# Layer 0's excess nodes: own rows by a product on TensorE in place of a gather from memory

## The chip, the core and the metric

The kernel runs on one core of one Trainium2 chip. The metric is the device time of one execution in microseconds (us). A core has engines that each work through a queue of their own, in order: PE (TensorE, matrix products), DVE (VectorE), ACT (ScalarE), POOL (GpSimd, which here mainly issues gathers) and SP (SyncE, which issues transfers). They wait for one another by semaphores. Matrix products land in PSUM[...]; everything else lies in SBUF, 128 partitions wide, or in device memory.

## The reference

Four graph-attention layers over the same graph of 3327 nodes with 256 features, each followed by a residual sum and a layer norm. A node has few neighbours (about 1% of the entries of the adjacency are set). Only layer 0 concerns the change:

```python
g_src = nodes @ W_src_w.T + W_src_b
g_tgt = nodes @ W_tgt_w.T + W_tgt_b
g = g_src[:, None, :] + g_tgt[None, :, :]
g = jax.nn.leaky_relu(g, NEG_SLOPE)
score = jnp.einsum('ijc,c->ij', g, a_w)
score = jnp.where(adj_mat != 0, score, -jnp.inf)
weights = jax.nn.softmax(score, axis=1)
return weights @ g_tgt
...
x = _layernorm(x + _L0_gnn_ref(x, adj, ...), axis=-1)
```

The leaky ReLU stands inside the sum over features, so a score needs all 256 features of both nodes. Layers 1 to 3 have scores that are sums of a term of each node, and are computed densely.

## The kernel before, in words

Layer 0 (`sparse0`) works on neighbour lists. The 26 tiles of 128 nodes are cut into four sets of 4, 7, 9 and 6 tiles (`SETS`). For each set, `neighbours(s)` reads the adjacency, encodes it by small products on PE into banks of the PSUM ring `v` (three banks, `fill`, L548), lets DVE pick the indices (`scan`, `sort`, L572 to L592), counts them and ranks the nodes of the set by degree (`ranks_i`, L682). Nodes are then taken in order of rank, so that tile 0 of a set has the nodes with most neighbours. For sets 1 to 3 the lists go to memory and back (`write_list` L731, `read_lists` L739, on POOL).

A node gets a number of seats, its tile's (`LEVELS`). Tile 0 would need 56 (`KMAX`), but has only 42 to 44 (`SEATS`); the neighbours over that are handled together, in one further part per set: the *excess*. Each of its 128 rows is a pair of a node and one of its neighbours over the seats. `excess(s)` (L760) gives every such pair a row, with comparisons on DVE (`seat`) and products on PE (L803) that carry along, for each row, the neighbour's index, the node's own index, its place in the tile and which of its seats it is. From these it makes `back` (row to node) and its transpose `forth` (node to row), both 128x128 matrices of zeros and ones.

The work is a list of parts: four seats of one tile make a part (`cuts_of`), tile after tile in the order 1, 0, 2, 3 and so on, with the excess part put in ahead of the last three parts of tile 0. There are 237 parts. One loop (L1282) goes over them. In step q it runs, in this order: some steps of the next set's `neighbours`; everything that `due` holds for q; the gathers of part q + 8 (`LEAD`); and the scores of part q. The order in which the loop calls is the order of each engine's queue (the manual schedule).

- `gather(q)` (L902): for every seat of the part, one indirect transfer on POOL fetches 128 table rows of 260 floats (`table_d`: projected target, with the score's linear part behind it) into a buffer `g`, one of a ring of 22. At a tile's beginning `gather_own` (L892) fetches the 128 nodes' own rows of 773 floats (minus the source projection at 0, the input at 257, the own target at 513) into `own`, of which there are four buffers. It is called 11 steps ahead of the tile's first part.
- `score(q)` (L942): DVE takes the larger of the gathered row and minus the source (L932), multiplies by the weight row `a_ps` and sums (L938).
- `weights` (L966): maximum on DVE, exponentials on ACT.
- `combine` (L1003), spread over the 8 steps after the tile's end: ACT scales each gathered row by its weight (L1012), PE adds the rows up by products with the identity (L1015). Then the `g` buffers are free.
- `add_input` (L1035), 10 steps after the tile's end: DVE divides and adds the input (L1041 to L1048), which is the last reading of the tile's `own`. `put_back` (L1054), 3 steps on: POOL writes the rows to memory in their old places.

For the excess, `gather_excess` (L828) issues two indirect transfers on POOL: own rows of 773 floats by the node's index, into one of the four `own` buffers, and table rows by the neighbour's index. `score_excess` (L841) takes the larger of the two on DVE (`y_over`, L845), weights and sums it. `send_scores` (L855), one step on, returns the scores to tile 0's seats by a product with `back`; later `send_weights` and `combine_excess` do the same for weights and rows.

In set 3's stretch no `neighbours` runs; there the ring `v` serves the first products of layer 1 for finished tiles (`early_bank`, `turn_next` L1139, `project_next` L1148). Layers 1 to 3 follow and overlap the end of layer 0 by a little.

Of the kernel before, what the change touches and what calls it, by code (L numbers as in the profile page):

```python
# [8 lines left out]
F32 = mybir.dt.float32  # L9
BF16 = mybir.dt.bfloat16  # L10
I32 = mybir.dt.int32
U32 = mybir.dt.uint32
U16 = mybir.dt.uint16
AF = mybir.ActivationFunctionType
ALU = mybir.AluOpType
# [4 lines left out]
P = 128  # L20
# [7 lines left out]
KMAX = 56  # L28
# [18 lines left out]
OWN = 773  # L47
# [3 lines left out]
def gat_stack(  # L51
# [29 lines left out]
    nc = tc.nc  # L81
    n, dim = x.shape
# [24 lines left out]
    table_d = dram.tile([n + 1, ROW], F32, name="table_d")  # L107
# [170 lines left out]
    def sparse0(lost):  # L278
        GROUP, TURNS, LEAD, SPREAD = 4, 22, 8, 8
        starts = [sum(SETS[:s]) for s in range(len(SETS))]  # L280
        with ExitStack() as s0:
            find = s0.enter_context(tc.tile_pool(name="s_find", bufs=2))
            const0 = s0.enter_context(tc.tile_pool(name="s_const", bufs=1))
            io0 = s0.enter_context(tc.tile_pool(name="s_io", bufs=2))
# [94 lines left out]
            upto = find.tile([P, P], F32, name="upto", bufs=1)  # L379
# [12 lines left out]
            minus_own = const0.tile([P, nt], F32, name="minus_own")  # L392
            nc.vector.tensor_scalar_mul(minus_own, own_i, -1.0)
            EXTRA = KMAX - min(SEATS.values())
            ramp = marks[:, 0, 0:1]
            before = find.tile([P, P], F32, name="before", bufs=1)
            given = find.tile([P, EXTRA, 4], F32, name="given", bufs=1)

            def excess_constants():
                nc.vector.tensor_scalar(before, upto, ramp, None, op0=ALU.is_gt)  # L400
                nc.vector.tensor_scalar(
                    given[:, :, 2], minus_own[:, 0:1].to_broadcast([P, EXTRA]), -1.0, 1.0,
                    op0=ALU.mult, op1=ALU.add,
                )
                nc.vector.tensor_scalar(given[:, :, 3], upto[:, :EXTRA], 1.0, None, op0=ALU.add)

            counts = const0.tile([P, nt, len(pieces) + 2], F32, name="counts")
            nc.vector.memset(counts, 0.0)
# [1 line left out]
            own_d = [  # L410
                dram.tile([size * P, OWN], F32, name=f"own{s}_d") for s, size in enumerate(SETS)
            ]
# [342 lines left out]
            held = {}  # L755
            between = []

            extras = {}

            def excess(s):  # L760

                lst, first = listed[s][:, 0, :], seats[s, 0]
                width = KMAX - first
                over = extras[s] = {}
                temp = a_ps[:, dim + 1 :]
                nc.vector.tensor_copy(given[:, :width, 0], lst[:, first:KMAX])
                nc.vector.tensor_copy(
                    given[:, :width, 1], lst[:, KMAX : KMAX + 1].to_broadcast([P, width])
                )
                there = io0.tile([P, EXTRA], F32, tag="there", name="there", bufs=1)  # L770
                count = io0.tile([P, 2], F32, tag="count", name="count", bufs=1)
                nc.vector.tensor_scalar(
                    there[:, :width], given[:, :width, 0], 0.0, 0.0, op0=ALU.is_gt, op1=ALU.add,
                    accum_out=count[:, 0:1],
                )
                absent = over["absent"] = io0.tile([P, EXTRA], F32, tag="absent", name="absent", bufs=1)
                nc.vector.tensor_scalar(
                    absent[:, :width], there[:, :width], -1.0, FAR, op0=ALU.add, op1=ALU.mult
                )
                yield  # L780
                nc.tensor.matmul(temp[:, 0:1], before, count[:, 0:1], start=True, stop=True)  # L781
                yield
                nc.vector.tensor_scalar(
                    count[:, 1:2], temp[:, 0:1], -float(BASE), None, op0=ALU.add
                )
                at = nt + starts[s]
                nc.vector.tensor_scalar(
                    lost[:, at : at + 1], count[:, 0:1], count[:, 1:2], float(P - BASE),
                    op0=ALU.add, op1=ALU.is_gt,
                )  # L790
                nc.vector.scalar_tensor_tensor(
                    there[:, :width], there[:, :width], float(BASE), upto[:, :width],
                    op0=ALU.mult, op1=ALU.add,
                )
                nc.vector.tensor_scalar(
                    there[:, :width], there[:, :width], count[:, 1:2], None, op0=ALU.add
                )
                for e in range(width):
                    seat = io0.tile([P, P], F32, tag="key_diag", name="seat")
                    nc.vector.tensor_scalar(  # L800
                        seat, upto, there[:, e : e + 1], None, op0=ALU.is_equal
                    )
                    nc.tensor.matmul(  # L803
                        temp[:, 8:12], seat, given[:, e, :], start=(e == 0), stop=(e == width - 1)
                    )
                    if e % 3 == 1:
                        yield
                yield
                taken = io0.tile([P, 4], F32, tag="taken", name="taken", bufs=1)
                nc.vector.tensor_copy(taken, temp[:, 8:12])  # L810
                rows = over["rows"] = io0.tile([P, 2], U32, tag="taken_i", name="taken_i", bufs=1)
                nc.vector.tensor_copy(rows, taken[:, :2])
                back = over["back"] = io0.tile([P, P], F32, tag="back", name="back", bufs=1)
                nc.vector.tensor_scalar(
                    back, upto, 1.0, taken[:, 2:3], op0=ALU.add, op1=ALU.is_equal
                )
                which = over["which"] = io0.tile([P, EXTRA], F32, tag="which", name="which", bufs=1)
                nc.vector.tensor_scalar(
                    which[:, :width], upto[:, :width], 1.0, taken[:, 3:4],
                    op0=ALU.add, op1=ALU.is_equal,  # L820
                )
                yield
                nc.tensor.transpose(temp[:, 96 : 96 + P], back, ident)
                yield
                there_too = over["forth"] = io0.tile([P, P], F32, tag="forth", name="forth", bufs=1)
                nc.scalar.copy(there_too, temp[:, 96 : 96 + P])

            def gather_excess(s, q):  # L828

                over = extras[s]  # L830
                own = over["own"] = io0.tile([P, OWN], F32, tag="own", name="own_of", bufs=4)
                g = over["g"] = gath.tile(
                    [P, GROUP, ROW], F32, tag=f"g{(q + SHIFT) % TURNS}", name="g"
                )
                for dst, src, x in ((own, own_d[s], 1), (g[:, 0, :], table_d, 0)):
                    nc.gpsimd.indirect_dma_start(
                        out=dst, out_offset=None, in_=src[:, :],
                        in_offset=bass.IndirectOffsetOnAxis(ap=over["rows"][:, x : x + 1], axis=0),
                    )

            def score_excess(s):  # L841

# [285 lines left out]
            def early_bank():  # L1128
                return ps0.tile([P, BANK], F32, tag="v", name="early", bufs=3)
# [50 lines left out]
            next(first)  # L1180
            score_columns()
            excess_constants()
            waiting, turns = None, 0
            for it in range(nt):
# [28 lines left out]
            def at_step(q, what, *args):  # L1213
                due.setdefault(q, []).append(lambda: what(*args))

            def once_placed(q, what, *args):
                due_gathers.setdefault(q, []).append(lambda: what(*args))

            due_gathers = {}
            for q, (key, k0, _) in enumerate(parts):  # L1220
                if k0 == KMAX:
                    at_step(q + 1, send_scores, key[0])
                    at_step(q + 2, take_scores, key[0])
                if k0 == 0:
                    if key[1] == orders[key[0]][0]:
                        at_step(q, judge, key[0])
                        at_step(q, lay_out, *key)
                    else:
                        once_placed(q - 3, gather_own, *key)
                        at_step(q - 2, lay_out, *key)  # L1230
# [15 lines left out]
            for s, q in begins.items():  # L1246
                work, at = excess(s), max(q - 2, 0)
                for y in range(12):
                    at_step(at + y, go_on, work)
# [48 lines left out]
            for q in sorted(due):  # L1298
# [7 lines left out]
                op0=ALU.mult, op1=ALU.add,  # L1306
# [777 lines left out]
    lost = nodes.tile([P, 2 * nt], F32, name="lost")  # L2084
    nc.vector.memset(lost, 0.0)
    rest = sparse0(lost)
    with ExitStack() as rs:
        layers(rs, EARLY, rest)
# [75 lines left out]
```

## Time and profile before

| | us |
|---|---|
| median of 3 timed runs (lowest to highest) | 3398.66 (3390.78 to 3407.27) |
| the profiled execution | 2952.55 |
| its span, first to last instruction | 2950.7 |

| engine | busy us | share of the span | instructions |
|---|---|---|---|
| PE (products) | 2317.0 | 79% | 15862 |
| DVE | 2134.7 | 72% | 5615 |
| POOL | 992.3 | 34% | 1061 |
| ACT | 852.4 | 29% | 2381 |

One execution was profiled, and all durations come from it. A share of the span is a mean over stages that differ, so it says little of any one of them. In the profile's rows `g<-table_d,lst` reads: an instruction that writes tile g from table_d and lst; x894 is how often; then come busy us, the mean ns of one, and the idle time of the engine before them with what ended it ("issue" is idle time in which nothing is waited for). L912 is line 912 of the program.

### The profile page before, as it was taken

To read this page: it belongs to the slowest core of one execution; us is meant where nothing else is said; L and a number is where in the kernel's file an instruction comes from. 1 tells how busy PE (TensorE), PEld (TensorE's weight loads), DVE (VectorE), ACT (ScalarE), POOL (GpSimd) and SP (SyncE) were. 2 spreads that over 40 slices of the span, in tenths; PEclk is the share of its full clock that TensorE was granted. 3 is DMA by queue.
4 is the path that set the end of the run, shared out by engine and by line. 5 is a ranking of instruction groups with operands and counts; after the bars stand their busy time and mean duration, and the time that the engine had idled before them with its cause. 6 is when DMAs were issued, how large, how long until landed. Compare 5 with 4: busy or idle time off the path is not lost.

```text
span 2950.7 us, 45073 instructions
## 1 busy us (share of the span) xinstructions
PE 2317.0 (79%) x15862; PEld 1359.2 (46%) x15862; DVE 2134.7 (72%) x5615; ACT 852.4 (29%) x2381; POOL 992.3 (34%) x1061
## 2 busy tenths in 40 slices
PE   7466667556545416657899999999999999999997
PEld 4222323222222103325688888763546567534332
DVE  6789789968776518755455521138999999999997
ACT  3244445434334304533344411110010110111211
POOL 2676767777777777772000000000000000000000
PEclk8576777777767757889999999999999999999998
DMA  7685655545644435545776733331222222212211
GB/s 234 194 263 147 187 166 171 141 130 158 166 112 114 112 107 124 171 120 165 227 208 195 201 82 107 110 98 45 73 61 84 75 80 63 73 43 62 59 47 48
DMA packets 183854, 370.50 MB, mean 126 GB/s; under 512 B 35772, under 2 KB 124707, under 8 KB 182596
## 3 DMA queue, kind: packets, MB, share of 16 engines
q1 hardware_dynamic: 103994, 178.49, 21.4%
q0 software_dynamic: 51008, 155.70, 19.1%
q10 hardware_dynamic: 28618, 33.33, 3.3%
q8 instruction: 128, 2.10, 0.3%
q14 instruction: 106, 0.87, 0.1%
HBM read 327.52 MB, written 46.23 MB: 127 GB/s over the span
## 4 chain that ended last, share of the span: by engine, by line
PE 46%; DVE 4%; DMA 2%; issue 0%; ACT 0%; SPq 0%; DVEq 0%; POOL 0%; POOLq 0%; ACTq 0%
PE acc L1773 18%; PE acc L1723 16%; PE acc L1781 9%; DVE e L1629 3%; PE misc L1557 3%; DMA at<-at_d 1%; PE misc L1666 0%; DMA at_d<-at 0%; DMA at_i<-in_adj_t_dram 0%; DVE stats L1952 0%; DVE h L1950 0%; DVE h L1745 0%; DVE both L1947 0%; PE misc L1822 0%; DMA dst<-in_l_att_dram 0%
## 5 line engine op out<-in xcount | busy, mean ns | idle before, releaser
L912 POOL DMA_INDIRECT g<-table_d,lst x894 | 851.6, 953 | 273.1 <-issue 245.6
L1629 DVE SCALAR_TENSOR_TENSOR e<-rate,feat,at 128x896 f32<-128x896 f32 (+4 forms) x832 | 843.6, 1080 | 59.2 <-PE acc L1781 47.7
L1015 PE MATMUL acc<-g,ident 128*128 128x512 f32 (+1 forms) x896 | 505.5, 708 | 262.3 <-ACT g L1012 246.1
L1773 PE MATMUL acc<-e,feat 128*32 128x384 f32 (+2 forms) x6656 | 692.7, 515 | 6.7 <-DVE h L1745 4.2
L1773 PEld LDWEIGHTS acc<-e,feat 128*32 128x32 f32 x6656 | 307.1, 110 | 300.2 <-issue 161.5
L1015 PEld LDWEIGHTS acc<-g,ident 128*128 128x128 f32 x896 | 195.1, 228 | 481.6 <-ACT g L1012 364.6
L1781 PE MATMUL acc<-e,feat 128*32 128x384 f32 (+3 forms) x3328 | 383.3, 512 | 0.0
L1012 ACT ACTIVATE g<-g,w 128x256 f32<-128x256 f32 x883 | 365.4, 495 | 0.4 <-ACT minus L489 0.4
L932 DVE TENSOR_TENSOR y<-g,minus_ps 128x1028 f32<-128x1028 f32 (+2 forms) x233 | 273.4, 1173 | 125.0 <-DMA g<-table_d,lst 115.9
L938 DVE SCALAR_TENSOR_TENSOR y<-y,a_ps 128x257 f32<-128x257 f32 x894 | 324.3, 418 | 24.8 <-PE a_ps L781 6.2
L1723 PE MATMUL acc<-feat,e 128*128 128x257 f32 (+2 forms) x1352 | 303.5, 382 | 9.1 <-DVE inv L1744 6.4
L1723 PEld LDWEIGHTS acc<-feat,e 128*128 128x128 f32 (+2 forms) x1352 | 254.9, 191 | 46.9 <-issue 9.3
L1723 PE MATMUL acc<-feat,at 128*128 128x257 bf16 (+2 forms) x2028 | 237.9, 274 | 4.2 <-DMA at<-at_d 4.0
L1781 PEld LDWEIGHTS acc<-e,feat 128*32 128x32 f32 (+1 forms) x3328 | 162.0, 110 | 130.8 <-issue 88.1
L1723 PEld LDWEIGHTS <-at 128*128 128x128 bf16 (+2 forms) x2028 | 198.8, 99 | 38.0 <-DMA at<-at_d 4.5
L553 PE MATMUL v<-code,leads 65*128 65x512 bf16 (+1 forms) x182 | 83.1, 458 | 156.9 <-DVE cand L579 111.0
L1629 DVE SCALAR_TENSOR_TENSOR e<-rate,feat,at_i 128x896 f32<-128x896 f32 (+2 forms) x104 | 112.3, 1081 | 92.1 <-DMA at_i<-in_adj_t_dram 44.6
L579 DVE MAX8 cand<-v 128x8 f32<-128x104 f32 (+2 forms) x858 | 158.9, 260 | 21.7 <-PE v L556 21.7
L1609 POOL DMA_DIRECT2D rate3b_d<-rate_rows x4 | 2.1, 520 | 449.8 <-ACT rate_rows L1608 449.8
L251 POOL TENSOR_TENSOR rstds<-rstds,minus_half 128x7 f32<-128x7 f32 (+1 forms) x8 | 12.0, 1506 | 385.0 <-DVE rstds L250 385.0
L1959 POOL TENSOR_TENSOR rstds<-rstds,minus_half 128x7 f32<-128x7 f32 (+1 forms) x4 | 7.6, 1912 | 384.5 <-DVE rstds L1958 384.5
L1656 ACT CAST at<-at_i 128x896 bf16<-128x896 int32 (+2 forms) x104 | 92.1, 885 | 111.9 <-DMA at_i<-in_adj_t_dram 75.5
(253 smaller groups left out, 1864.6 us busy)
## 6 DMA issues: line engine op xcount, KB each, us to landing
adj_i<-in_adj_dram SPq DMA_DIRECT2D x75, 512.0 KB
at<-at_d SPq DMA_DIRECT2D x150, 224.0 KB
at_i<-in_adj_t_dram SPq DMA_DIRECT2D x50, 448.0 KB
at<-at_d SPq DMA_DIRECT2D x75, 192.0 KB
at<-at_d SPq DMA_DIRECT2D x75, 191.8 KB
g<-table_d,lst POOLq DMA_INDIRECT x894, 2.8
at_d<-at ACTq DMA_DIRECT2D x50, 224.0 KB
at_i<-in_adj_t_dram SPq DMA_DIRECT2D x25, 384.0 KB
```

Of the source, the lines that this page charges most:

```text
L579: nc.vector.max(spread[:, c0 + c, :], view(v[:, :w]))
L912: nc.gpsimd.indirect_dma_start(out=g[:, k - k0, :], out_offset=None, in_=table_d[:, :], in_offset=bass.IndirectOffsetOnAxis(ap=entry["lst" ...
L932: nc.vector.tensor_tensor(y, rows, minus_src[:, None, :].to_broadcast([P, m, dim + 1]), op=ALU.max)
L938: nc.vector.scalar_tensor_tensor(y, y, 1.0, a_ps[:, : dim + 1], op0=ALU.mult, op1=ALU.mult, accum_out=sc)
L1012: nc.scalar.activation(rows, rows, AF.Copy, scale=w[:, k : k + 1])
L1015: nc.tensor.matmul(dst, ident, rows, start=start, stop=stop)
L1557: nc.tensor.matmul(pacc[:pn, : dim + self.extra], ht[:, k, :pn], self.weight[:, k, :], start=(k == 0), stop=(k == kc - 1),)
L1629: nc.vector.scalar_tensor_tensor(e[:pn, : c1 - c0], self.rate[b][:pn, h_of, : c1 - c0], q, at[:pn, : c1 - c0], op0=ALU.max, op1=ALU.mult,)
L1656: nc.scalar.copy(at[:pn, :w], at_i[:pn, :w])
L1723: nc.tensor.matmul(accs[s][:pn, : dim + 1], a[:pj, s * P : s * P + pn], f[:pj, : dim + 1], start=(j == 0 and part == 0), stop=(j == nt - 1 ...
L1773: nc.tensor.matmul(accs[x][p][q : q + 32, : hi - lo], f[:pj, at0 : at0 + 32], es[at0 // hd][:pj, lo:hi], start=(j == 0), stop=(j == nt - 1),)
L1781: nc.tensor.matmul(accs[x][pairs][h_of * 32 : (h_of + 1) * 32, : hi - lo], f[:pj, dim + h_of : dim + h_of + 1].to_broadcast([pj, 32]), es[ ...
```

## The change

The own rows of the excess pairs already lie on chip: they are rows of tile 0's `own`. The change drops their gather. A new function `send_own` lets PE multiply `forth` with the first 257 columns of tile 0's `own`, into a bank of the ring `v`; `score_excess` reads them from there. It is called one step ahead of the excess part. The node's own index need no longer be carried through the seat products, so `given`, `taken` and `rows` lose a column. `gather_excess` keeps the transfer of table rows. Nothing else is edited.

```diff
-            given = find.tile([P, EXTRA, 4], F32, name="given", bufs=1)
+            given = find.tile([P, EXTRA, 3], F32, name="given", bufs=1)
...
                 nc.vector.tensor_copy(given[:, :width, 0], lst[:, first:KMAX])
-                nc.vector.tensor_copy(
-                    given[:, :width, 1], lst[:, KMAX : KMAX + 1].to_broadcast([P, width])
-                )
...
                     nc.tensor.matmul(
-                        temp[:, 8:12], seat, given[:, e, :], start=(e == 0), stop=(e == width - 1)
+                        temp[:, 8:11], seat, given[:, e, :], start=(e == 0), stop=(e == width - 1)
                     )
...
-                rows = over["rows"] = io0.tile([P, 2], U32, tag="taken_i", name="taken_i", bufs=1)
-                nc.vector.tensor_copy(rows, taken[:, :2])
+                rows = over["rows"] = io0.tile([P, 1], U32, tag="taken_i", name="taken_i", bufs=1)
+                nc.vector.tensor_copy(rows, taken[:, 0:1])
...
             def gather_excess(s, q):
 
                 over = extras[s]
-                own = over["own"] = io0.tile([P, OWN], F32, tag="own", name="own_of", bufs=4)
                 g = over["g"] = gath.tile(
                     [P, GROUP, ROW], F32, tag=f"g{(q + SHIFT) % TURNS}", name="g"
                 )
-                for dst, src, x in ((own, own_d[s], 1), (g[:, 0, :], table_d, 0)):
-                    nc.gpsimd.indirect_dma_start(
-                        out=dst, out_offset=None, in_=src[:, :],
-                        in_offset=bass.IndirectOffsetOnAxis(ap=over["rows"][:, x : x + 1], axis=0),
-                    )
+                nc.gpsimd.indirect_dma_start(
+                    out=g[:, 0, :], out_offset=None, in_=table_d[:, :],
+                    in_offset=bass.IndirectOffsetOnAxis(ap=over["rows"][:, :1], axis=0),
+                )
+
+            def send_own(s):
+
+                over = extras[s]
+                over["own"] = early_bank()
+                nc.tensor.matmul(
+                    over["own"][:, : dim + 1], over["forth"], held[s, 0]["own"][:, : dim + 1],
+                    start=True, stop=True,
+                )
...
                 if k0 == KMAX:
+                    at_step(q - 1, send_own, key[0])
                     at_step(q + 1, send_scores, key[0])
                     at_step(q + 2, take_scores, key[0])
```

More of the change, by code (lines that the diff above doesn't have):

```diff
@@ L401, in excess_constants @@
                 nc.vector.tensor_scalar(
-                    given[:, :, 2], minus_own[:, 0:1].to_broadcast([P, EXTRA]), -1.0, 1.0,
+                    given[:, :, 1], minus_own[:, 0:1].to_broadcast([P, EXTRA]), -1.0, 1.0,
                     op0=ALU.mult, op1=ALU.add,
                 )
-                nc.vector.tensor_scalar(given[:, :, 3], upto[:, :EXTRA], 1.0, None, op0=ALU.add)
+                nc.vector.tensor_scalar(given[:, :, 2], upto[:, :EXTRA], 1.0, None, op0=ALU.add)
             counts = const0.tile([P, nt, len(pieces) + 2], F32, name="counts")
@@ L808, in excess @@
                 yield
-                taken = io0.tile([P, 4], F32, tag="taken", name="taken", bufs=1)
-                nc.vector.tensor_copy(taken, temp[:, 8:12])
-                rows = over["rows"] = io0.tile([P, 2], U32, tag="taken_i", name="taken_i", bufs=1)
-                nc.vector.tensor_copy(rows, taken[:, :2])
+                taken = io0.tile([P, 3], F32, tag="taken", name="taken", bufs=1)
+                nc.vector.tensor_copy(taken, temp[:, 8:11])
+                rows = over["rows"] = io0.tile([P, 1], U32, tag="taken_i", name="taken_i", bufs=1)
+                nc.vector.tensor_copy(rows, taken[:, 0:1])
                 back = over["back"] = io0.tile([P, P], F32, tag="back", name="back", bufs=1)
                 nc.vector.tensor_scalar(
-                    back, upto, 1.0, taken[:, 2:3], op0=ALU.add, op1=ALU.is_equal
+                    back, upto, 1.0, taken[:, 1:2], op0=ALU.add, op1=ALU.is_equal
                 )
@@ L818, in excess @@
                 nc.vector.tensor_scalar(
-                    which[:, :width], upto[:, :width], 1.0, taken[:, 3:4],
+                    which[:, :width], upto[:, :width], 1.0, taken[:, 2:3],
                     op0=ALU.add, op1=ALU.is_equal,
```

## The prediction, on record ahead of the changed kernel's run

> **What bounds the kernel now.** I read the page's slices first, then a table of stretches, then the instructions of the gather queue (POOL) in order of time, because the change takes four instructions out of that queue.
>
> The page's part 2, one digit for each of 40 slices of 74 us:
>
> ```profile
> PE   7466667556545416657899999999999999999997
> ...
> DVE  6789789968776518755455521138999999999997
> ...
> POOL 2676767777777777772000000000000000000000
> ```
>
> Two programs stand one after the other. In the first 18 slices (layer 0) POOL is never above 7 and never idle; from slice 20 PE is full and POOL is empty. The change is in the first. A 7 on POOL does not look like a bound; the next three views show that it is one. The stretches (columns: stretch, length, then busy us and instructions of PE, PE's loads, DVE, ACT, POOL; granted clock, DMA share, GB/s):
>
> ```profile
> 300.00:400.00 100.00, 65.16 (x167) 29.45 (x165) 76.82 (x351) 37.73 (x98) 70.97 (x75) 0.74 0.61 178
> 400.00:500.00 100.00, 66.96 (x165) 29.16 (x166) 95.91 (x405) 55.81 (x146) 72.69 (x76) 0.77 0.59 170
> 600.00:700.00 100.00, 54.76 (x133) 24.96 (x133) 72.59 (x306) 33.77 (x90) 75.89 (x80) 0.70 0.50 139
> 1000.00:1100.00 100.00, 22.43 (x41) 9.38 (x40) 25.91 (x87) 16.47 (x43) 76.23 (x80) 0.62 0.40 106
> ```
>
> From 500 us on POOL starts 80 instructions in every 100 us, whether DVE is 73% or 26% busy: one in 1.25 us. The group of the gathers (page, part 5) and the view of who waited for whom (total us, times, longest) say the same:
>
> ```profile
> L912 POOL DMA_INDIRECT g<-table_d,lst x894 | 851.6, 953 | 273.1 <-issue 245.6
> ```
> ```profile
> DVE y L932 <- DMA g<-table_d,lst: 115.9, 55, 4.9
> ```
>
> 953 ns of work and 0.30 us of issue between two (245.6 us over 807 of them) make the 1.25 us, and DVE, which scores the gathered rows, waits for gathers 55 times. None of these waits lies between 120 and 550 us: there DVE sets the pace, and after 550 us POOL does. So what counts is every place where POOL stands still before 550 us and every slot in its queue after. In order of time, between its first gather at 87 us and its last at 1343.5 us, its long stops (over 1.2 us) are three, the last columns being the idle time before the instruction and who ended it:
>
> ```profile
> 226.59 0.95 POOL L897 DMA_INDIRECT own_of<-own_d,lst  x1 [3.50 <-DVE y_over L845]
> ...
> 262.73 1.00 POOL L731 DMA_INDIRECT lists_d<-payload,ranks_i  x1 [9.15 <-DVE ranks_i L682]
> ...
> 391.31 0.95 POOL L836 DMA_INDIRECT own_of<-own_d,taken_i  x1 [0.30 <-DVE cand L579]
> 392.57 0.95 POOL L836 DMA_INDIRECT g<-table_d,taken_i  x1 [0.30 <-issue]
> 404.38 0.95 POOL L897 DMA_INDIRECT own_of<-own_d,lst  x1 [10.86 <-DVE hs L1041]
> ```
>
> The reader is to see who is waited for. Both own_of stops are waits for a buffer: `own` has four, and the excess rows (L836) take one of them. At 226.59 the own rows of set 0's tile 3 want the buffer that the excess of set 0 holds until DVE's y_over; at 404.38 those of set 1's tile 2 want the buffer of set 0's tile 3, which `add_input` (L1041, DVE, 403.62 us) reads last. From 404 us to the last gather POOL never stops again, apart from two short instructions of its own. The chain of waits then runs from the end of layer 0 (acc L1015 at 1362.28, the last sums_d at 1368.28, an SP load at 1372.62, layer 1's matmuls from 1383.07) to the end of the program, so a layer 0 that ends earlier carries through.
>
> **What the Trainium skill says.** "Perfetto Trace Analysis", section "DMA Instruction — SWDGE (GPSIMD)": a POOL DMA's record ends when its descriptors are made, not when the data lands. The trace agrees: own rows of 773 floats take POOL 949 ns and table rows of 260 floats 953 ns, so an instruction removed is worth one slot, whatever its bytes. "VectorE: DVE Perf Modes", section "The perf-mode tier table (the rule you actually need)": `tensor_tensor` in fp32 runs at its base rate from SBUF and from PSUM alike. The trace agrees: the max at L932 with its second operand in PSUM takes 414 ns at 128x257, the one at L845 from SBUF 410 ns.
>
> **The change part by part.**
>
> Removed from POOL: four gathers at L836 (176.9, 391.3, 740.9, 1158.2 us), 1.25 us each, 5.0 us of queue. The first lies before the stop at 262.73, which ends when DVE has the ranks of set 1; that DVE work waits for no gather, so the slot is only waited out there: 0. The other three count, the one of 391.3 together with the stop behind it.
>
> Removed with it: one of the users of the four `own` buffers. In the changed program the own gather of set 0's tile 3 takes a buffer that nobody has used, and that of set 1's tile 2 takes the buffer of set 0's tile 2, whose last reader (L1048 of that tile ends at 342.9 us) is 50 us past. In the built program's order neither gather waits for DVE any more. So both own_of stops go. The 3.50 us lie before 262.73 and are waited out there: 0. Of the 10.86 us I ask what is late next. Without the stop and without L836, POOL would be 12.1 us early. Two things stop it again. The `put_back` of set 0's tile 3 (413.18 us before) needs L1048, which ends at 405.08: it can come 8.1 us early. The gather of set 1, tile 2, part 0 (422.0 us before) needs the buffer of 22 parts earlier, which PE's first combining products of set 1's tile 1 free:
>
> ```profile
> 410.17 3.78 PE L1015 MATMUL acc<-g,ident 128*128 128x512 f32 x4 [10.27 <-ACT g L1012]
> 413.74 1.06 PE L1015 MATMUL acc<-own_of,ident 128*128 128x256 f32 x2
> ```
>
> These end at 413.95, so it can start at about 414.0: 8.0 us early. After that the buffers are freed 10 to 60 us before they are wanted, and the ranks of set 2 (576.5 us for a use at 599.2) and the moments at L1092 (478.1 for 513.8) leave room. So this stop is worth 8.0 us, not 12.1.
>
> The gathers at 740.9 and 1158.2 lie where POOL is the bound: 2 x 1.25 = 2.5 us.
>
> Added to PE: four `send_own` products, 128x128 by 128x257, in fp32. The nearest row is L452, whose two such products take 1.03 us at 420.16 and 2.05 us at 357.67 under a lower clock: 0.5 to 1.0 us each, 2 to 4 us in all, on a PE that is 50 to 67% busy there: 0. They take a bank of the `v` ring (three), so the next fills of the neighbour search come later: in set 0 the fill that ran at 219.69 now needs the scan that ends at 226.0. DVE wants that bank only after y_over, its weighting and a scan (about 2.0 us), and the fill takes about 1.1: between 0 and 1 us lost, I take 0.2, once; in sets 1 to 3 DVE has room against POOL. Behind `send_own` on PE stand combining products and fills; for it waits DVE's y_over. In set 3 PE is late (DVE's hs L1041 waits 13.3 us for acc there, right behind y_over), so y_over takes over that wait and hs finds it over: 0.
>
> DVE: four casts L767 of 172 ns go (0.7 us, of which those of the DVE-paced stretch are 0.3), the copies of 4 and 2 columns become 3 and 1: under 0.1. The max reads PSUM in place of SBUF: 0. These and the lost 0.2 cancel. The seat products go from 4 columns to 3 (296 ns either way). DMA: 4 x 128 x 3092 B = 1.6 of 370.5 MB: 0.
>
> Sum: 8.0 + 2.5 = 10.5, less 0.2 for rounding of the hand-over to layer 1: 10.3 us. In the profiled execution 2952.55 us (span 2950.7) becomes 2942.3. The timed runs have a median of 3398.66 (3390.78 to 3407.27), 446 us above the profiled one, and the trace does not show where these lie. I carry the saving over in us, since the POOL queue's own pace depends on no other engine: 3398.66 - 10.3 = **3388.4**, 0.3%. A measurement of this kernel tells about 0.5% (17 us) from no change.
>
> **The rivals.**
> 1. *The full release* (0.32). PE frees the buffer at 414 only in this execution; in the timed ones the DVE-paced stretch and its stops are probably longer too. If both own_of stops and all four slots count in full: 14.36 + 5.0 = 19.4 us, **3379**, to 3372 if the stops are half as long again. For it: the timed run is 15% longer. Against: the stops before 262.73 must be waited out.
> 2. *Nothing arrives* (0.11). POOL's start at 264 depends on DVE, and if DVE or PE pace the stretch of 404 to 600 us in the timed runs, the lead is eaten: between 0 and 2.5 us, **3398**. For it: DVE is 96% busy at 400:500. Against: DVE's waits for gathers from 550 us on.
> 3. *Slower: y_over behind PE's queue* (0.15). `send_own` stands in PE's order behind combining products that wait for ACT's scaled rows, 15.1 us at the longest (PE's load waiting for g L1012). If it is that late at set 0, DVE waits 15.1 us where it sets the pace, and the ranks of set 1 and all behind them move by as much. The bank taken out of the ring can at the worst double what DVE loses on fills in 85 to 265 us, 6.9 us in six waits. With 2.5 us of queue saved: 15.1 + 6.9 - 2.5 = +19.5, **3418**. It decides from where the loss in set 0 exceeds the 10 us gained. Against: at 218.73 PE had only a 1.10 us wait for ACT, and `send_own` stands before that product.
> 4. That the change does not do what it says needs the gathers still in the queue; the built order has 257 POOL rows for 261, so I give it nothing of its own.
>
> **How the numbers follow.** Forecast 0.42, rivals 0.32, 0.11, 0.15. The forecast's own range is 3382 to 3396 with the runs' spread of 8 us either way. The range of all is 3368 to 3414: it takes in the full release with longer stops and leaves out most of rival 3. Faster by over 0.5% (below 3381.7): nine tenths of rival 1 and a fifth of the forecast, 0.29 + 0.09 = 0.38. Slower (above 3415.7): most of rival 3, 0.13. Within: 0.49.
>
> **What would show it.** The stop at 404.38 is gone, and POOL stops instead near 401 to 414 us for 3 to 5 us, waiting for DVE's hs or PE's acc; the last gather stands near 1333 instead of 1343.5; L897 has no wait above 0.4 us after the first; y_over is not waited for in set 0. If DVE waits for the new product by more than 2 us in set 0, or the last gather is at 1341 or later, I am wrong.

## The result, and the profile after

| | kernel before | changed kernel | ratio, 95% interval |
|---|---|---|---|
| first comparison, 7 runs each | 3398.66 us (3390.78 to 3410.72) | 3373.02 us (3353.66 to 3378.81) | 0.9922 [0.9897, 0.9947] |
| the profiled execution | 2952.55 us (span 2950.7) | 3353.66 us (span 3351.9) | not comparable, see below |

The change saves 25.6 us, 0.78%; forecast were 10.3 us. The time, 3373, lies within the range stated for all cases (3368 to 3414), but outside the forecast's own (3382 to 3396): it is rival 1's, 3379 to 3372 us.

The two profiles can't be laid side by side: the one of before took 446 us less than its timed runs; the one of the changed kernel took what its timed runs take. The page's slices of the changed kernel (40, of 84 us each; lines left out are marked by three dots here and below):

```profile
PE   6156355444254433445459999999999999999997
...
DVE  6278457567276654444464555210689999989997
...
POOL 2733644555645656655620000000000000000000
```

In the profile that the forecast was worked out from, POOL stood at 6 or 7 through layer 0; here it stands mostly at 3 to 6, layer 0 takes 20 slices of 84 us in place of 18 of 74, and no engine is fuller for it. The table of stretches of the changed kernel (columns as in the prediction: stretch, length, busy us and instructions of PE, its loads, DVE, ACT, POOL; clock, DMA share, GB/s):

```profile
300.00:400.00 100.00, 40.30 (x94) 17.09 (x95) 61.86 (x243) 29.93 (x79) 52.33 (x55) 0.65 0.38 102
400.00:500.00 100.00, 56.55 (x139) 26.33 (x142) 58.04 (x264) 37.92 (x98) 54.07 (x57) 0.69 0.47 136
600.00:700.00 100.00, 52.83 (x122) 23.91 (x124) 67.99 (x284) 41.05 (x108) 58.82 (x62) 0.75 0.44 121
1000.00:1100.00 100.00, 43.89 (x105) 18.95 (x107) 59.15 (x243) 34.63 (x90) 58.83 (x62) 0.70 0.50 132
```

POOL starts 55 to 62 instructions per 100 us, not 75 to 80. A gather still takes 953 ns (`L916`, in the page's groups), so POOL's instructions are not slower; it stands still more often. Nor are the transfers slower: a packet of POOL's transfers in layer 0 takes 169 ns in the mean, as in the profile of before. A lower TensorE clock hardly makes up the 365 us that layer 0 takes longer: the granted share is 0.67 in it (0.73 before), and PE is busy for 711 us, against 706. What the engines wait for is told by the view of who waited for whom (total us, times, longest) and by a piece of the order in time; "remote" is a releaser that the profile can't name:

```profile
DVE y L942 <- remote: 138.0, 30, 9.2
...
PE v L553 <- remote: 78.3, 7, 25.9
...
DVE found L587 <- remote: 40.9, 13, 9.5
```

```profile
380.58 0.95 POOL L916 DMA_INDIRECT g<-table_d,lst  x1 [0.30 <-issue]
380.96 0.33 DVE L584 MAX8 cand<-cand 128x8 f32<-128x165 f32 x1 [8.89 <-remote]
...
380.98 0.61 PE L553 MATMUL v<-code,leads 65*128 65x512 bf16 x1 [8.69 <-remote]
```

L584 reads `cand`, which DVE itself has just written, and the only signal that it waits for is DVE's own that the write is done. The write ended at 372.06 us, the next signal on that semaphore is on record at 380.93, and DVE ran nothing in between. So an engine waited 8.89 us for itself, and PE waited with it. In the profile of before, and in every profile below with a span under 2960 us, none of these groups has a wait on "remote". The changed kernel's DVE has 2791 instructions that give a signal. The trace of this execution has 2531 such signals on record, and after 333 of the 2791 none came within 1 us of the instruction's end; in a 2939 us execution of the same kernel (e5 below), 2792 are on record, and it was so for 1. The Trainium skill, "DMA: Bandwidth & Descriptors", section "Why a DMA increments its semaphore by 16 and not by 1", says that a DMA which POOL issues gives 16 signals. The trace of before agrees: 1032 POOL transfers and 16,521 signals on their semaphores. The changed kernel's first profile has 3,662 for 1028 transfers. So signals come late there. Whether the missing ones were merged with others or only left out of the records, and what holds them up, the records don't show.

POOL's stops are mostly waits for other engines that are late themselves. From its first gather of own rows to its last gather it stops for over 4 us in 37 places, against 4 in that 2939 us execution: at 17 of the 26 `put_back`s, mostly for DVE's hs, at 14 gathers into `g` buffers, and longest of all at the gather of the first excess part, whose indices are not there yet:

```profile
218.41 0.95 POOL L831 DMA_INDIRECT g<-table_d,taken_i  x1 [43.88 <-DVE taken_i L809]
```

Whether the kernel takes the short time or the long one goes with the chip. The runs below were made in six groups on five chips: on two of these (call them kind F) the kernel before takes 2950 to 2955 us, on three (kind L) 3376 to 3396, and all runs of a group are of one kind. Only one chip was used twice, and it was of kind F both times; that something else which lasts as long as a group decides it, and not the chip, is not ruled out. By their times the first profile of before is of kind F, the timed runs of the first comparison and the changed kernel's profile are of kind L; which chips these ran on is not on record. So the forecast was worked out from one kind and compared on the other.

### The profile page after: what moved, and what is told of

The parts are those of the page before. It is cut to its first block, busy times and chain, and to the rows that moved or that the text cites. A ratio compares the mean times of both kernels' runs of the same rounds, so it can differ in the third digit from the quotient of the medians.

```text
span 3351.9 us, 45053 instructions
## 1 busy us (share of the span) xinstructions
PE 2356.7 (70%) x15849; PEld 1369.6 (41%) x15870; DVE 2142.4 (64%) x5611; ACT 855.1 (26%) x2381; POOL 988.9 (30%) x1057
## 4 chain that ended last, share of the span: by engine, by line
PE 47%; DVE 17%; issue 12%; another core or an unknown queue 11%; POOL 8%; DMA 3%; ACT 3%; ACTq 0%; DVEq 0%; POOLq 0%; SPq 0%
PE acc L1778 16%; PE acc L1728 14%; PE acc L1786 8%; POOL g L916 6%; PE acc L1019 4%; DVE y L942 4%; DVE y L936 3%; DVE e L1634 2%; PE misc L1562 2%; DVE cand L579 2%; ACT g L1016 1%; DVE found L587 1%; DVE cand L589 1%; DMA g<-table_d,lst 1%
## 5 line engine op out<-in xcount | busy, mean ns | idle before, releaser
L916 POOL DMA_INDIRECT g<-table_d,lst x894 | 851.8, 953 | 409.5 <-issue 283.6
L1019 PE MATMUL acc<-g,ident 128*128 128x512 f32 (+1 forms) x896 | 539.7, 745 | 380.0 <-ACT g L1016 304.4
L1019 PEld LDWEIGHTS acc<-g,ident 128*128 128x128 f32 x896 | 202.2, 238 | 617.7 <-ACT g L1016 386.6
L553 PEld LDWEIGHTS <-leads 65*128 65x128 bf16 x182 | 22.5, 124 | 313.9 <-DVE cand L579 136.9
L251 POOL TENSOR_TENSOR rstds<-rstds,minus_half 128x7 f32<-128x7 f32 (+1 forms) x8 | 12.1, 1508 | 387.9 <-DVE rstds L250 387.9
```

What stands on the lines that cost most here:

```text
L553: nc.tensor.matmul(v[:, :w], leads[:, b, :], code[:, :w], start=True, stop=False)
L916: nc.gpsimd.indirect_dma_start(out=g[:, k - k0, :], out_offset=None, in_=table_d[:, :], in_offset=bass.IndirectOffsetOnAxis(ap=entry["lst" ...
L1019: nc.tensor.matmul(dst, ident, rows, start=start, stop=stop)
```

## The experiments

Each was timed beside the kernel before on the same chip; its median stands in brackets.

| run | edit | chip kind | us (before) | ratio, 95% interval |
|---|---|---|---|---|
| e1_before_again | the kernel before, unchanged | F | 2951.52 (2949.61) | 1.0004 [0.9995, 1.0012] |
| e2_ring_free | before, ring of `own` freed, gathers kept | F | 2942.08 (2949.61) | 0.9977 [0.9967, 0.9988] |
| e3_slot_back | changed, with four gathers that nobody reads | F | 2940.70 (2949.61) | 0.9968 [0.9955, 0.9981] |
| e4_after_three | changed, three `own` buffers | F | 2949.17 (2949.61) | 0.9997 [0.9989, 1.0005] |
| e5_after_again | the changed kernel again | F | 2939.54 (2954.61) | 0.9949 [0.9937, 0.9961] |
| e6_product_alone | before, with the product added | F | 2951.49 (2954.61) | 0.9990 [0.9981, 0.9998] |
| e7_put_late | changed, put_back 2 steps later | F | 2944.12 (2954.61) | 0.9965 [0.9952, 0.9978] |
| e8_root_act | changed, three roots moved off POOL | L | 3367.90 (3377.26) | 0.9974 [0.9960, 0.9987] |
| e9_after_third | the changed kernel again | L | 3373.13 (3396.44) | 0.9924 [0.9894, 0.9955] |
| e10_ring_free_2 | as e2 | L | 3361.25 (3375.81) | 0.9949 [0.9935, 0.9963] |
| e11_before_third | the kernel before, unchanged | F | 2949.26 (2950.82) | 0.9996 [0.9989, 1.0004] |
| e12_slot_back_2 | as e3 | F | 2941.56 (2950.82) | 0.9965 [0.9951, 0.9979] |

**The kernel before again (e1, e11), and the changed kernel again (e5).**

> The kernel before, unchanged. It is run for a second profile, since the first one (span 2950.7 us) lies 446 us below the timed runs, while the changed kernel's (3351.9) lies at its own. If the short profile was one odd execution: span near 3390 us, with stops on DVE of 5 to 10 us between dependent instructions in layer 0 like those in the changed kernel's profile (47 DVE stops over 2.5 us before 1710 us, against 24 in the first profile). If the kernel before is profiled short for a reason of its own: span near 2950 again. Time: 3399 us, ratio 1.000, whatever holds.

> The kernel before, unchanged, for a profile of it in the condition of the first comparison (if this job's runs have it, near 3377 to 3399 us). Theory B: both own_of stops stand in it, the one of set 1's tile 2 and that of set 0's tile 3, and together they are longer than the 14.4 us of the first profile, by what the gain is longer: 20 to 30 us; further own gathers wait as well. If own_of stops are no longer than 15 us in all, the surplus comes from elsewhere. Ratio 1.000.

> The changed kernel, unchanged, beside the kernel before in the condition that this job's runs have. If the kernel before runs near 2950 us here: theory A (the forecast's sum, 10.3 us, holds in the condition it was worked out in; the slots are worth what lies between this run and the one with the slots back, 2940.7) gives 2939 us, ratio 0.9965; theory B 2930 us (0.9934); theory D (the saving is a share of the time, 0.78% as in the first comparison) 2927 us (0.992). If the kernel before runs near 3399 us here: 3373 again, 0.992.

Both repeats of before landed on F chips: 2951.52 and 2949.26 us. The short profile was no odd execution, the chip was of the other kind. e11 was meant for a profile of before on an L chip; none was had, so that profile is missing here.

e5 is the case that the forecast's sum was made for. Its stops of POOL between 215 and 440 us, in order of time (start, length, instruction, and in brackets the idle time before it and who ended it):

```profile
243.75 0.95 POOL L916 DMA_INDIRECT g<-table_d,lst  x1 [6.75 <-PE acc L1019]
...
260.15 1.00 POOL L731 DMA_INDIRECT lists_d<-payload,ranks_i  x1 [9.16 <-DVE ranks_i L682]
...
402.76 1.00 POOL L1061 DMA_INDIRECT sums_d<-hs,lst  x1 [4.27 <-DVE hs L1052]
```

and its stretches:

```profile
400.00:500.00 100.00, 70.19 (x173) 31.31 (x174) 95.87 (x406) 58.34 (x153) 73.78 (x78) 0.78 0.59 171
...
1000.00:1100.00 100.00, 21.67 (x40) 8.90 (x38) 29.44 (x101) 14.41 (x38) 75.92 (x81) 0.60 0.39 105
```

Both own_of stops are gone; in place of the 10.86 us stands one of 4.27 that waits for DVE's hs in the put_back of set 0's last tile, as the prediction said. The stop for set 1's ranks is as long as before (9.16 against 9.15), so what POOL gains ahead of it is waited out: before it a stop of 6.75 us for a `g` buffer has taken the place of the 3.50.

In time, e5 is 15.1 us below the kernel before beside it (11.5 to 18.6 by the interval) and 11.3 us below the kernel before beside e11 (2950.82, same chip, another group of runs). The forecast for this kind was 2942.3; e5 took 2939.54 (2936.43 to 2943.37). That is near theory A's 2939 us, but A's ratio of 0.9965 lies just outside the interval, and B's and D's do too. The traces below account for about 8 us of the gain. Some 3 us of the 15.1 may lie in the runs beside it: e6, which only adds work, came out 3.1 us below the same runs of the kernel before. Where the remainder comes from is not shown.

**The ring freed alone (e2, e10).**

```diff
-                own = over["own"] = io0.tile([P, OWN], F32, tag="own", name="own_of", bufs=4)
                 g = over["g"] = gath.tile(
                     [P, GROUP, ROW], F32, tag=f"g{(q + SHIFT) % TURNS}", name="g"
                 )
+                own = over["own"] = g[:, 1:4, :].rearrange("p a b -> p (a b)")[:, :OWN]
```

> The kernel before, with its four gathers of own rows kept, but landing in the three unused quarters of the excess part's own g buffer, so that the ring of four own buffers has one user fewer, as in the changed kernel. Theory A (the forecast: buffer wait 8.0 us, queue slots 2.5 us): 3391 us, ratio 0.998. Theory B (the buffer waits are longer in the timed runs and are nearly the whole gain): 3376 us, ratio 0.993. Theory C (the gathers taken out of the queue are the gain, some 6 us each, and the ring is nothing): 3399 us, ratio 1.000.

> The kernel before with its four gathers of own rows landing in the excess part's g buffer, once more, for the condition of the first comparison (kernel before near 3377 to 3399 us). There the changed kernel gains 0.76 to 0.78%, about 25 us. Theory B (the ring's waits are what grows when signals come late): at least two thirds of it, 17 us or more, ratio 0.995 or less. Theory C for that condition (the queue slots, the descriptors and signals of four gathers grow): 0.998 to 1.000. Where the kernel before runs near 2950 us: 0.9977 again.

The excess part uses one quarter of its `g` buffer; the own rows fit into the other three. On the F chip (e2), POOL's stops in the same stretch:

```profile
243.61 0.95 POOL L912 DMA_INDIRECT g<-table_d,lst  x1 [3.22 <-PE acc L1015]
...
259.99 1.00 POOL L731 DMA_INDIRECT lists_d<-payload,ranks_i  x1 [9.14 <-DVE ranks_i L682]
...
402.64 1.00 POOL L1057 DMA_INDIRECT sums_d<-hs,lst  x1 [3.05 <-DVE hs L1048]
```

From the first write of set 1's lists to this put_back POOL needs 402.64 - 259.99 = 142.65 us. In the profile of before the put_back stands here:

```profile
413.18 1.00 POOL L1057 DMA_INDIRECT sums_d<-hs,lst  x1 [0.30 <-issue]
```

That is 413.18 - 262.73 = 150.45 us, and it is 150.48 and 150.33 in e1 and e11; in e5, 402.76 - 260.15 = 142.61. So the freed buffer is worth 7.8 us here, with the gathers in the queue or without; the forecast said 8.0. The time says 7.5 (2949.61 - 2942.08). Theory A holds, B and C fall on this kind of chip.

On an L chip (e10) the same edit gives 0.9949: 17 us by this ratio (12.5 to 21.9 by the interval), 14.6 by the medians. It is more than on the F chip, where the interval is 3.5 to 9.7. By the ratio it is two thirds of the changed kernel's 0.76 to 0.78%, just what theory B asked for at the least; by the medians it is less than B's 17 us, and the two edits were timed on different L chips.

**The slots put back (e3, e12).**

```diff
-                nc.gpsimd.indirect_dma_start(
-                    out=g[:, 0, :], out_offset=None, in_=table_d[:, :],
-                    in_offset=bass.IndirectOffsetOnAxis(ap=over["rows"][:, :1], axis=0),
-                )
+                for k in (1, 0):
+                    nc.gpsimd.indirect_dma_start(
+                        out=g[:, k, :], out_offset=None, in_=table_d[:, :],
+                        in_offset=bass.IndirectOffsetOnAxis(ap=over["rows"][:, :1], axis=0),
+                    )
```

> The changed kernel, with one more gather of table rows in the excess part, into an unused quarter of its g buffer, read by nobody: the four POOL instructions are back, the own ring stays free and the product stays. Theory A: 3373 + 2.5 = 3376 us (ratio to the kernel before 0.993). Theory B: 3373 + 5 = 3378 us or less (0.994). Theory C: all is given back, 3399 us (1.000).

> The changed kernel with the four queue slots filled by gathers that nobody reads, for the condition of the first comparison. The ring freed by itself gave 0.9949 there and the changed kernel 0.9924. If the slots are the rest: this run lies near the ring freed alone, 0.995. If not: near the changed kernel, 0.9925. Near 2950 us before: 0.9968 again.

Theory C is out, since most of the gain stays. How much is given back, the times don't tell: 1.2 and 2.0 us by the medians against e5, but 0.0019 and 0.0016 by the ratios, some 5 us, with intervals that overlap. The traces tell more. From the first write of set 1's lists to the last gather POOL takes 1071.7 us in e5, 1072.0 in e3 and e12, 1072.2 in e2, and 1079.8 to 1080.5 in the three profiles of before: the slots are worth 0.3 to 0.5 us there, not the 2.5 of the forecast. From that put_back to the start of the last gather e3 needs 1333.34 - 403.85 = 929.49 us and e5 1331.83 - 402.76 = 929.07, though e5 has two instructions fewer there. The changed kernel's POOL stops in between; e5 between 590 and 630 us, and its last gather:

```profile
598.43 0.96 POOL L916 DMA_INDIRECT g<-table_d,lst  x1 [1.20 <-issue]
...
606.07 0.99 POOL L731 DMA_INDIRECT lists_d<-payload,ranks_i  x1 [1.61 <-DMA lists_d<-payload,ranks_i]
...
622.66 0.99 POOL L731 DMA_INDIRECT lists_d<-payload,ranks_i  x1 [1.63 <-DMA lists_d<-payload,ranks_i]
...
1331.83 0.96 POOL L916 DMA_INDIRECT g<-table_d,lst  x1 [0.30 <-issue]
```

e3 has only the one near 606 (its put_back stands before it, its last gather behind):

```profile
403.85 1.00 POOL L1062 DMA_INDIRECT sums_d<-hs,lst  x1 [2.64 <-DVE hs L1053]
...
606.11 0.99 POOL L731 DMA_INDIRECT lists_d<-payload,ranks_i  x1 [1.44 <-DMA lists_d<-payload,ranks_i]
...
1333.34 0.95 POOL L917 DMA_INDIRECT g<-table_d,lst  x1 [0.30 <-issue]
```

Beyond the usual 0.30 us, all longer stops from the put_back to the last gather come to 3.55 us in e5 and 1.16 in e3 (1.36 in the kernel before, e11): 2.4 of the two slots' 2.5 us are lost again. Some 1.5 of these lie at the writes of set 2's lists, where a write waits for the one before it to land, and 0.9 at the gather at 598.43, for which the profile names no wait. These are small times read from single executions (e12 has 1.5 us of such stops, with the slots back), so the place of the loss is less sure than its size. There is no run of this edit on an L chip.

**A tighter ring (e4).**

```diff
-                own = entry["own"] = io0.tile([P, OWN], F32, tag="own", name="own_of", bufs=4)
+                own = entry["own"] = io0.tile([P, OWN], F32, tag="own", name="own_of", bufs=3)
```

> The changed kernel with three own buffers in place of four: the four gathers stay out, but an own gather now waits for the last reading of the tile three before, as tight as the kernel before is in its two places, and in more places. Theories A and B: the gain of the ring is lost and more: at least 3391 us for A (0.998), at least 3394 for B (0.999), rather above 3399. Theory C: 3373 us, no change against the changed kernel (0.992).

```profile
226.72 0.95 POOL L901 DMA_INDIRECT own_of<-own_d,lst  x1 [8.28 <-DVE hs L1045]
...
339.21 0.95 POOL L901 DMA_INDIRECT own_of<-own_d,lst  x1 [7.68 <-DVE hs L1045]
...
401.39 0.95 POOL L901 DMA_INDIRECT own_of<-own_d,lst  x1 [4.48 <-DVE hs L1045]
```

With the slots out and buffer stops back, two at the same own gathers as in before and one at the gather of the tile between them (339.21), the whole gain is gone (0.9997). It agrees with e2 from the other side: the buffer is what counts. That the loss comes out just as large as the gain is chance, since the stops are one more and of other lengths.

**The product alone (e6).** The own gathers stay, with the ring held until y_over by a copy of one column; the product is added (`send_own` as in the change).

```diff
-                own = over["own"] = io0.tile([P, OWN], F32, tag="own", name="own_of", bufs=4)
+                own = over["fetched"] = io0.tile([P, OWN], F32, tag="own", name="own_of", bufs=4)
...
+                nc.vector.tensor_copy(weight[:, 1:2], over["fetched"][:, 0:1])
...
+                    at_step(q - 1, send_own, key[0])
```

> The kernel before with the new product added and read by y_over from PSUM, while the four gathers of own rows stay in the queue and in the ring of own buffers, held until y_over by a one-column copy on DVE. Only what the change adds, nothing that it takes away. Theory A (product hidden on PE, 0.2 us for the bank): 2950 us, ratio 1.000. Rival 3 of the forecast (y_over waits behind PE's queue, the bank delays the fills): slower by 2 us or more, up to 22, ratio 1.001 to 1.007.

0.9990, so the addition costs nothing that shows; rival 3 is out on this kind of chip. The own_of stops stand there as in before (2.79 and 9.87 us). Where y_over is waited for in the changed kernel (e5, the view of the tiles `early` and `y_over`, the four products in two passes each):

```profile
L840 PE MATMUL early<-own_of,forth x8: 380/542/767, 214.9 to 1180.0; 128*128 128x257 f32 x8
```

```profile
L849 DVE TENSOR_TENSOR y_over<-g,early x4: 402/403/425, 223.3 to 1180.4; 128x257 f32<-128x257 f32 x4
...
  PE early L840: 11.4, 1
```

One wait of 11.4 us, at 1180 us, in set 3. In the profile of before DVE's hs waited 13.31 us for PE's acc right behind that place, and of that wait 1.91 us are left in e5. The line of before:

```profile
1192.84 0.48 DVE L1041 SCALAR_TENSOR_TENSOR hs<-acc,inv,own_of 128x256 f32<-128x256 f32 x1 [13.31 <-PE acc L1015]
```

It is the same lateness of PE, met a little earlier, as the prediction had it. In the profiles on L chips y_over is waited for in set 3 alone too (27.2 us in the first, 28.6 in e9).

**put_back later (e7).**

```diff
-                at_step(q + 13, between.append, lambda key=key: put_back(*key))
+                at_step(q + 15, between.append, lambda key=key: put_back(*key))
```

> The changed kernel with put_back two steps later (15 after a tile's end in place of 13). What is left of the stop near 410 us is 2.8 us of waiting for DVE's hs by the put_back of set 0's last tile. If that wait alone holds POOL there: 1 to 3 us faster than the changed kernel, 2937 us (0.9958). If the g buffer that PE frees at the same time takes over (theory A named both): no change, 2939 us (0.9965). If the later put_back delays the moments of a set: slower than 2941.

```profile
411.98 0.95 POOL L916 DMA_INDIRECT g<-table_d,lst  x1 [4.52 <-PE acc L1019]
```

The stop for hs is gone and one of the same length for the `g` buffer has come, six gathers later: the prediction's two next-late things, one behind the other. The ratio is 0.9965 against the changed kernel's 0.9949, no gain. The median is 4.6 us above e5's and above the 2941 that the expectation gave to a third case, moments that come late; the intervals overlap, and whether that case holds was not followed up.

**The roots off POOL (e8).**

```diff
             def finish_root(s):
                 rstd = moments[s][1][:, : SETS[s]]
-                nc.gpsimd.tensor_tensor(
-                    rstd, rstd, minus_half.to_broadcast([P, SETS[s]]), op=ALU.pow
-                )
+                if s == len(SETS) - 1:
...
+                    return
+                nc.scalar.activation(rstd, rstd, AF.Sqrt)
+                nc.vector.reciprocal(rstd, rstd)
```

> The changed kernel with three more instructions taken out of POOL's queue: the roots of the layer norm of sets 0 to 2 (L1101, 1.45 us each by the profile, 0.30 to issue) go to ACT (Sqrt, with a change of table there and back) and DVE (reciprocal). It measures what a slot is worth after 410 us. Theory A (POOL's queue is the bound there, so that a slot counts in full; the forecast's second term, which the changed kernel showed only in part): 3 x 1.75 = 5.2 us below the changed kernel, 2934 us where the kernel before takes 2952 (ratio 0.994). If the lists of set 2 (ranks_i on DVE, which POOL waits for near 617 and 633 us) take over, only the one or two roots behind them count: 1.7 to 3.5 us, 2936 to 2938 (0.995). Where this job's runs of the kernel before are near 3399 us: 3373 - 5 = 3368 us or less (0.991).

Set 3 keeps its root on POOL. The run landed on an L chip, where three slots fewer than the changed kernel give 0.9974: 9.4 us by the medians, less than the changed kernel shows on another chip of that kind (e9), and the intervals don't meet. On an F chip, where the slot's price was the question, it was not tried, so it is no better version. Either the six table loads that ACT has more (1.28 us each in its trace) and the two more hand-overs between engines cost there what the slots save and more, or chips of kind L differ among themselves by more than such an edit is worth (the kernel before takes 3376 and 3377 us on two of them, 3396 on the third); these runs don't tell which.

**The changed kernel on an L chip again (e9).**

> The changed kernel once more, for its gain in whichever condition this job's runs of the kernel before show. Near 2950 us before: theory A 2939 us (0.9962), as the first repeat's profile says (11.5 us shorter); 0.9949 again would say that the gain there is nearer 15. Near 3377 to 3399 us before: if the signals that come late there make the two lost waits dearer (theory B), a ratio near 0.992 again, 25 us; if the first comparison's surplus over 10 us was spread between few runs (its runs lie within 20 us either way), 0.997, 10 us; and then no more than the kernel with the roots moved as well (0.9974).

0.9924, 23.3 us by the medians: the surplus over 10 us is there again on another chip, and not a matter of few runs. Its stretches, as in the first profile of the changed kernel:

```profile
400.00:500.00 100.00, 54.10 (x136) 25.12 (x138) 57.63 (x259) 33.41 (x86) 53.67 (x57) 0.68 0.47 137
...
1000.00:1100.00 100.00, 42.02 (x94) 17.90 (x94) 57.61 (x235) 29.64 (x78) 54.08 (x58) 0.66 0.44 118
```

## Why the prediction was right, and where it was off

- *Direction and mechanism: right, shown on F chips.* Of the two things taken away, the buffer counts and the slots hardly do. The stop at 404.38 went, a shorter one for hs came in its place (4.27 us, forecast 3 to 5), then the `g` buffer (e7). Of the signs that the prediction named, e5 also has the last gather where it should be (it ends at 1332.8 us, forecast 1333), no wait of an own gather after the first, and none of y_over in set 0.
- *The number: luck in part.* The forecast's own sum was 10.3 us. The measured time falls into the stated range because that range took in rival 1; it lies 9 us below the forecast's own.
- *Term "8.0 us for the stop": right on F chips.* 7.8 us in the traces of e2 and e5, 7.5 in e2's time. (The 10.86 us of the stop, and so the "12.1 us early" and rival 1's 14.36, hold the usual 0.30 us of issue as well; the 8.0 doesn't rest on it.)
- *Term "2.5 us for two slots": too large by the traces.* It is 0.3 to 0.5 us there; the times leave anything from 1 to 5 open. The prediction took POOL as the bound without a break from 404 us on, and wrote that "the ranks of set 2 ... leave room". But it had looked at the ranks only, not at the list writes behind them: in e5 two of these wait for the one before to land, and lose 1.5 us more than in e3.
- *Added product and bank, 0.2 us: right on F chips.* e6 costs nothing that shows, and y_over waits only in set 3 and for the most part in place of hs. Rival 3 did not come.
- *The step that failed: "I carry the saving over in us, since the POOL queue's own pace depends on no other engine".* In the timed runs of the comparison POOL's pace does depend on others: 57 instructions in 400 to 500 us in place of 76 to 78, with DVE and PE waiting for signals that come late, and POOL for DVE and PE. On such chips the freed ring alone is worth 14.6 us by the medians (e10) in place of 7.5, and the change 23 to 26 in place of 11 to 15. Rival 1 named this ("the DVE-paced stretch and its stops are probably longer too") and its time is what was measured, though it did not know of the late signals; its other half, that both stops and all slots count in full, is not so on F chips, where the stop ahead of set 1's ranks is waited out.
- *Open:* the kernel before was never profiled on an L chip, so where its 14.6 us of ring waits lie there, and whether the remaining 10 us are slots, transfers or differences between chips, is not shown.
- The likeliest case put the time within 0.5% of before; it came to 0.78% faster.

## What to carry to other kernels

A transfer that is taken out of a queue may be worth less for its slot than for the buffer that it no longer borrows: look who shares the ring, and try the buffer by itself, by letting the data land in an idle part of another one. Then ask of every such gain what is late next, also hundreds of microseconds on, where an earlier queue meets waits that the old one never saw. And when the profiled execution is far from the timed ones, a saving need not carry over in microseconds; settle that difference first, since other waits may rule the timed runs.

## What was not expected of the hardware

- One program, two kinds of chips, as far as five chips tell: 2950 to 2955 us against 3376 to 3396, with nearly all the difference in the first, gather-bound part. In the first profile of before the last gather starts at 1342.57 us (of 2950.7), in e9's at 1716 (3362.2); what follows takes 1608 and 1646 us.
- On the slower kind an engine waits up to 9 us for its own signal (8.89 us for L584, whose input DVE had just written), and of 16 signals for each gather under 4 are on record. The gather's own duration is unchanged, 953 ns in both.
- What an edit gains there is not the sum that the faster kind shows: the same freed buffer gave 0.23% on one and 0.51% on the other, by the ratios.
